# Softmax sums taken by ScalarE from the scores of the maxima, instead of by GpSimd and TensorE from the weights

## The chip, the core and the metric

One core of a Trainium2 chip runs the whole kernel. The metric is the device time of one execution in microseconds; the kernel before takes 1525.75 us (median of three runs, 1524.82 to 1526.85). The five engines each work through their own queue in order: TensorE (PE; its weight loads are listed as PEld), VectorE (DVE), ScalarE (ACT), GpSimd (POOL) and SyncE (SP), which here issues most transfers. TensorE writes its results into eight PSUM banks of 128 partitions by 512 float32 numbers.

## What is computed

```python
def reference(x, wq, wk, wv, wo, A, B, Wr, br):          # x: 4 x 1024 x 512, float32
    q, k, v = (x @ w.T as 16 heads of 32, for w in (wq, wk, wv))
    probs = softmax(einsum('bqhd,bkhd->bhqk', q, k))      # over the 1024 keys, no scaling
    x = layernorm(x + einsum('bhqk,bkhd->bqhd', probs, v) @ wo.T)
    logits = x @ Wr.T + br                                # 8 experts, the best one is taken
    h, y = einsum('nd,erd->ner', x, A), einsum('ner,eor->neo', h, B) / 64
    return layernorm(x + y[best expert] * softmax(logits)[best expert])
```

Four batches of 1024 tokens go through attention with 16 heads, a layer norm, a choice of one of eight experts of rank 64 for each token, and a second layer norm. All is float32. The softmax needs, for each query and head, the maximum of 1024 scores, the exps of the scores less that maximum (the weights), and the sum of these exps. The change is about where that sum is taken.

## The kernel before

The work is cut into units of one batch and four heads (32 columns each, so four heads fill 128 partitions): 16 units. Scores are made twice, in two layouts.

*For the maxima* (`scores`, L280): a step takes 128 queries and 512 keys, that is one half of the keys, of one unit. Four matmuls (L290), one for each head, write four banks with the queries on partitions, and VectorE reduces each bank to 128 negated maxima (L292). Every eight such steps fill a tile `top` of 2 x 128 queries x 4 heads x 2 halves; the smaller of the two negated maxima is taken (L296), GpSimd splits it into three bfloat16 parts (`split`, L190), which it writes into three of every 32 columns of the tile `spread_m`, and TensorE turns that tile (`turn_m`, L299), so that ScalarE can copy `mT` out: maxima on partitions, queries along the row.

*For the weights* (`weigh`, L313): 16 steps later, a step takes 256 queries and 256 keys of a unit, with the keys on partitions. In each of four banks, one matmul with ones (L321) spreads the negated maxima and two matmuls (L330) add the scores. ScalarE's exp (L340) turns the four banks into weights, `probs`. Here the keys lie on partitions, so a sum over keys goes across them: GpSimd adds the eight tiles of keys up into `dens` (L343, L351), all but the last one (or two).

*At the end of four steps* the 1024 keys of a chunk of 256 queries are done. `combine` (L364) multiplies the weights by the values into one bank (L372), and ScalarE copies it into half of a tile `both` (L380). Two steps later `settle` (L383) sums `dens` and the last weights across partitions by matmuls with ones (L360), and ScalarE copies that into the other half (L391); VectorE takes reciprocals (L394) at the end of that step and a step later GpSimd multiplies the halves (`divide`, L399) into `aT`, which the output projection needs.

The order on every engine is the order in which the program is written (`keep_order`). Step i of the loop at its end emits: transfers (`early`), small things that must come first (`ahead`), the weights of step i - 16, the scores of step i, the combine if step i - 16 ends a chunk (such steps are called `busy`), small work due at that step (`small`), the pieces that a planner has put there (`fill`) and small things that come last (`behind`). There are 256 + 16 steps. Weights and scores therefore run side by side in 240 of them; the first 16 have scores only and the last 16 weights only.

The planner (L913) deals out the pieces: projections to q, k and v of later units, each into one bank (`project_q`, `project_k`, `project_v`, copied out by ScalarE), the output projection with the first norm (`After.project`, `norm`), the experts (`After.step`; for the last batch `Last.up`, `mask`, `down`) and their norms. Costs are in TensorE columns: a step without a combine has 4 * 512 + 512 + 4 * 512 = 4608, a combine 8192, half a projection 4096. Pieces are added to a step that is not busy while its length and half the next piece stay below a level, which is at least `SHORTEST` = 8800 and more where deadlines (`last`) ask for it. Windows `first` and `last` say when a piece may and must run.

`bank()` gives out the eight banks in turn, whoever asks. A matmul into a bank waits until what was in it has been read.

`apply` (L419) is the second half of a layer norm, one ScalarE instruction with a scale and a bias for each partition, for 128 tokens of 512 numbers.

Of the kernel before, what the change touches and what calls it, by code (L numbers as in the profile page):

```python
# [41 lines left out]
def attention_then_experts(  # L42
# [89 lines left out]
    before_f = work.tile([P, P], F32, tag="both", name="before_f")  # L132
# [34 lines left out]

    spread_m = [const.tile([P, HT, GH, HD], BF16, tag=f"sm{i}", name=f"sm{i}") for i in range(2)]
# [3 lines left out]
    expand_f = work.tile([E, E, R], F32, tag="dens", name="expand_f")  # L172
# [36 lines left out]
    qT, kT, vS, mT, aT, top, probs, dens = {}, {}, {}, {}, {}, {}, {}, {}  # L209
# [43 lines left out]
    def project_q(u, x):  # L253

        ps = bank()[:, :QC]
        for c in range(C):
            pe.matmul(ps, wq_sb[:, c, ts(units[u][1], P)], x.x[:, c, :], start=(c == 0), stop=(c == C - 1))  # L257
        qT[u, x.n] = work.tile([P, QC], F32, tag="q", name="q", bufs=3 * NQ)
        act.copy(qT[u, x.n], ps)

    def project_k(u, x):

        if x.n == 0:
            kT[u] = work.tile([P, S], F32, tag="k", name="k", bufs=5)
        ps = bank()[:, :QC]
        for c in range(C):
            pe.matmul(ps, wk_sb[:, c, ts(units[u][1], P)], x.x[:, c, :], start=(c == 0), stop=(c == C - 1))  # L267
        act.copy(kT[u][:, ts(x.n, QC)], ps)

    def project_v(h, x, t):  # L270

        if x.n == 0 and t == 0:
            vS[x.b, h] = work.tile([P, NK, H2 + E], F32, tag="v", name="v", bufs=3)
        ps = bank()[:, : H2 + (E if h else 0)]
        for c in range(C):
            pe.matmul(ps, x.x[:, c, ts(t, P)], wv_sb[:, c, columns(h)], start=(c == 0), stop=(c == C - 1))  # L276
        act.copy(vS[x.b, h][:, x.n * TQ + t, : H2 + (E if h else 0)], ps)


    def scores(s):  # L280

        u, t, n = maxima[s]
        i, here = divmod(s, TS)
        if here == 0:
            top[i] = work.tile([P, HT, GH, 2], F32, tag="top", name="top")
        tiles = [bank() for _ in range(GH)]
        q = qT[u, t // TQ]
        for j, ps in enumerate(tiles):
            r = slice(j * HD, (j + 1) * HD)
            pe.matmul(ps, q[r, ts(t % TQ, P)], kT[u][r, ts(n, 512)], start=True, stop=True)  # L290
        for j, ps in enumerate(tiles):
            dve.tensor_reduce(top[i][:, here // 2, j, n : n + 1], ps, axis=AX.X, op=ALU.max, negate=True)  # L292
        if here == TS - 1:
            m = work.tile([P, HT, GH], F32, tag="m", name="m")
            parts = [spread_m[i % 2][:, :, :, p] for p in range(NP)]
            dve.tensor_reduce(m, top[i], axis=AX.X, op=ALU.min)  # L296
            split(m, parts, "mrest")
# [15 lines left out]
    def weigh(s):  # L313
# [27 lines left out]
        if kp == 0:  # L341
            dens[u, c] = work.tile([P, GH * QC], F32, tag="dens", name="dens")
            pool.tensor_add(  # L343
                dens[u, c],
                pr[:, 0].rearrange("p j q -> p (j q)"),
                pr[:, 1].rearrange("p j q -> p (j q)"),
            )
        else:
            for k in range(2):
                if 2 * kp + k < added(u):  # L350
                    pool.tensor_add(dens[u, c], dens[u, c], pr[:, k].rearrange("p j q -> p (j q)"))  # L351

    def added(u):

        return NK - 1 if u < U - 1 else NK - 2

    def sum_up(ps, tiles):
        for i, w in enumerate(tiles):
            for j in range(GH):
                pe.matmul(  # L360
                    ps[j * HD : (j + 1) * HD, :], ones, w[:, j, :], start=(i == 0), stop=(i == len(tiles) - 1)
                )

    def combine(u, c):  # L364

        b, g = units[u]
        ps = bank()
        v = vS[b, g // 2]
        for k in range(NK):
            for j in range(GH):  # L370
                col = (g % 2) * P + j * HD
                pe.matmul(  # L372
                    ps[j * HD : (j + 1) * HD, :QC],
# [5 lines left out]
        both = work.tile([P, 2 * QC], F32, tag="both", name="both")  # L379
        act.copy(both[:, :QC], ps[:, :QC])  # L380
        return both

    def settle(u, c, both):  # L383

        ps = bank()[:, :QC]
        sum_up(
            ps,
            [probs[u, c, k // 2][:, k % 2] for k in range(added(u), NK)]
            + [dens[u, c].rearrange("p (j q) -> p j q", q=QC)],
        )  # L390
        act.copy(both[:, QC:], ps)  # L391

    def invert(both):
        dve.reciprocal(both[:, QC:], both[:, QC:])  # L394

    def divide(u, c, both):
        b, g = units[u]
        aT[b, g, c] = work.tile([P, QC], F32, tag="aT", name="aT", bufs=16)
        pool.tensor_mul(aT[b, g, c], both[:, :QC], both[:, QC:])  # L399
# [19 lines left out]
    def apply(h, rs, i):  # L419
        act.activation(h, h, AF.Identity, bias=rs[:, 1, i : i + 1], scale=rs[:, 0, i : i + 1])  # L420
# [234 lines left out]
    class Last:  # L655
# [26 lines left out]
        def norm(self):  # L682
            for i in range(TQ):
                apply(self.h[i], self.rs, i)
# [63 lines left out]
    COST_S, COST_T, COST_AV = 4 * 512, 512 + 4 * 512, 4 * NK * QC  # L748
    HALF = 4 * C * QC
    SHORTEST = 8800  # L750
# [33 lines left out]
    summed = {}  # L784
    for i, (u, c, kp) in enumerate(weights):
        if kp == KP - 1:
            later(i + NS + 2, 2048, lambda u=u, c=c: settle(u, c, summed[u, c]))
            later(i + NS + 2, 0, lambda u=u, c=c: invert(summed[u, c]), where=behind)
            later(i + NS + 3, 0, lambda u=u, c=c: divide(u, c, summed[u, c]))
# [4 lines left out]
    for i in range(len(weights) // TS):  # L794
        later(TS * i + TS + 2, 512, turn_m, i)


    for u in range(1, LAST):
        for n in range(NQ):
            x_in = Load(units[u][0], n)  # L800
            first = max(start_of(u - 3) + KP * (n + 1), 0)
# [32 lines left out]
    for b, r in enumerate(rest):  # L834
# [7 lines left out]
        for t in range(NT):  # L842
            n, i = divmod(t, TQ)
            for half in range(2):
                then = []
                if i == TQ - 1 and half == 1:
                    then = [(2, 0, r.norm, n), (3, 0, r.choose, n), (4, 0, r.gate, n)]
                    if n == NQ - 1:
                        then += [(4, 600, r.count)]
                        then += [(5 + k // 4, 0, r.scatter, k) for k in range(NT)]  # L850
# [3 lines left out]
                    end - NS + KP * (n + 1) + 3,  # L854
                    end - NS + KP * (n + 1) + 8,
# [4 lines left out]
        for k in range(NT + 2):  # L860
# [3 lines left out]
                end + 14 + 3 * k,  # L864
                end + 21 + 3 * k,
                after=[(p, 3 if k else 9)],
                then=[(-1, 0, r.weigh_y, k - 2), (2, 0, r.norm_y, k - 2), (3, 0, r.store, k - 2)] if k >= 2 else [],
# [12 lines left out]
    for n in range(NQ):  # L880
        a = start_of(LAST) + NS * n + NS - 1
        p, ups, downs = None, [], []
        for i in range(TQ):
            for half in range(2):
                then = []
                if i == TQ - 1 and half == 1:
                    gap = 2 if n < NQ - 1 else 1
# [6 lines left out]
                    a + 4,  # L894
                    a + 9 if n < NQ - 1 else a + 5,
# [4 lines left out]
        for k in range(C):  # L900
            ups.append(Piece(on_last(n, "up", k), HALF, a + 8, a + 16, after=[(p, gap + 2)]))
        q = Piece(on_last(n, "mask"), 1024, a + 10, a + 18, after=[(p, gap + 3)] + [(o, 1) for o in ups])

        first = a + 12 if n != NQ - 2 else N + 5
        for i in range(TQ):
            for half in range(2):
                done = i == TQ - 1 and half == 1
                then = [(1, 0, on_last(n, "finish"))] if done else []
                Piece(on_last(n, "down", i, half), HALF, first, a + 22, after=[(q, 1)], then=then)
# [84 lines left out]
    for i in range(len(base)):  # L994
# [8 lines left out]
        if i in busy:  # L1003
            u, c, _ = weights[i - NS]
            summed[u, c] = combine(u, c)
# [43 lines left out]
```

## Time and profile before

| | |
|---|---|
| median of three runs | 1525.75 us |
| the profiled execution | 1532.2 us |
| its span, first to last instruction | 1530.5 us, granted TensorE clock 0.997 |
| first weights / last scores on TensorE | 99.8 us / 1407.8 us |
| PE busy | 1495.6 us (98%) |
| POOL busy | 1116.1 us (73%), of it the adds into dens 896.2 |
| DVE busy | 929.0 us (61%), of it the maxima 635.0 |
| ACT busy | 763.2 us (50%), of it the exps 528.8 |
| mean time of one multiply or add of 256 columns out of a bank by VectorE (L457) | 421 ns |
| mean time of one copy of 256 columns out of a bank by ScalarE (L380) | 373 ns |

A group of the profile gives line, engine, operation, tile written and tile read, shapes and count; then the busy time and the mean time of one in ns; then the idle time of the engine just before them and what ended it. A window line gives, for one stretch, the busy time and number of instructions of each engine (PE, PEld, DVE, ACT, POOL in this order), the granted clock and the DMA engines' share. A timeline line gives start, length, engine, line and operation, with equal neighbours merged. A busy TensorE counts pipelined matmuls whose ends are modelled, so instructions of one engine may overlap.

### The profile page before, as it was taken

What the parts mean: (1) busy time and instruction counts of PE and PEld (TensorE: products, weight loads), DVE (VectorE), ACT (ScalarE), POOL (GpSimd) and SP (SyncE); (2) the same over time, 40 slices, a digit from 0 to 9 for tenths busy, and PEclk for the clock granted to TensorE, in tenths of its full rate; (3) what the DMA queues carried; (4) which work ended last, traced back from release to release, by engine and by line L of the source; (5) the groups of instructions that cost most, each with busy time, mean ns of one, the idle gap of its engine ahead of it and who ended that gap; (6) DMA issues with size and microseconds to landing.
All of it is one profiled execution on the core that took longest, in us unless ns stands there. A gap on an engine that the chain in (4) does not pass through costs nothing.

```text
span 1530.5 us, 37870 instructions
## 1 busy us (share of the span) xinstructions
PE 1495.6 (98%) x15571; PEld 965.1 (63%) x15571; DVE 929.0 (61%) x1733; ACT 763.2 (50%) x1583; POOL 1116.1 (73%) x939
## 2 busy tenths in 40 slices
PE   8999999999999999999999999999999999999996
PEld 6666666666666666666666666666666565665655
DVE  1556666656676457666677556766667567776323
ACT  1125555554445556555445555655445455555551
POOL 2028888877777777888777868888877777778880
PEclk9999999999999999999999999999999999999999
DMA  7431212132002423324100522441400331121000
GB/s 234 138 102 51 71 43 71 42 97 99 15 15 97 146 84 111 113 90 146 35 15 30 173 84 77 125 139 43 166 15 16 123 93 33 57 82 61 29 1 28
DMA packets 93054, 122.13 MB, mean 80 GB/s; under 512 B 7608, under 2 KB 68040, under 8 KB 92881
## 3 DMA queue, kind: packets, MB, share of 16 engines
q1 hardware_dynamic: 84672, 103.93, 21.6%
q0 software_dynamic: 6096, 13.69, 2.4%
q8 instruction: 122, 2.00, 0.6%
q10 hardware_dynamic: 2112, 2.10, 0.4%
q14 instruction: 52, 0.42, 0.1%
HBM read 92.34 MB, written 33.63 MB: 82 GB/s over the span
## 4 chain that ended last, share of the span: by engine, by line
PE 88%; POOL 4%; ACT 3%; issue 2%; DVE 2%; DMA 1%; ACTq 0%; POOLq 0%; SPq 0%; DVEq 0%
PE bank L372 14%; PE bank L290 14%; PE bank L330 13%; PE bank L276 8%; PE bank L257 8%; PE bank L267 8%; PE bank L455 7%; PE bank L321 5%; PE bank L360 4%; POOL dens L351 3%; ACT probs L340 2%; PE bank L601 2%; PE bank L617 2%; PE bank L608 2%; PE bank L729 1%
## 5 line engine op out<-in xcount | busy, mean ns | idle before, releaser
L292 DVE TENSOR_REDUCE top<-bank 128x1 f32<-128x512 f32 x1024 | 635.0, 682 | 458.9 <-PE bank L290 451.9
L351 POOL TENSOR_TENSOR dens<-dens,probs 128x1024 f32<-128x1024 f32 x316 | 745.3, 2358 | 128.7 <-ACT probs L340 116.4
L340 ACT ACTIVATE probs<-bank 128x512 f32<-128x512 f32 x1024 | 528.8, 603 | 286.2 <-PE bank L330 272.9
L290 PE MATMUL bank<-k,q 32*128 32x512 f32 x2048 | 287.1, 594 | 1.5 <-DVE whose_i L552 1.3
L330 PE MATMUL bank<-q,k 32*128 32x256 f32 x4096 | 266.9, 374 | 0.0
L372 PE MATMUL bank<-probs,v 128*32 128x256 f32 x4096 | 236.0, 381 | 0.8 <-ACT probs L340 0.8
L330 PEld LDWEIGHTS bank<-q,k 32*128 32x128 f32 x4096 | 201.4, 184 | 18.8 <-issue 3.2
L372 PEld LDWEIGHTS bank<-probs,v 128*32 128x32 f32 x4096 | 127.1, 110 | 125.9 <-ACT probs L340 47.9
L343 POOL TENSOR_TENSOR dens<-probs 128x1024 f32<-128x1024 f32 x64 | 150.9, 2358 | 62.7 <-ACT probs L340 62.4
L257 PE MATMUL bank<-xT,wq 128*128 128x256 f32 x512 | 129.2, 398 | 8.7 <-DMA xT<-in_xt 6.1
L290 PEld LDWEIGHTS bank<-k,q 32*128 32x128 f32 x2048 | 112.0, 184 | 25.8 <-issue 6.1
L267 PE MATMUL bank<-xT,wk 128*128 128x256 f32 x512 | 125.4, 389 | 1.4 <-ACT probs L340 0.9
L276 PE MATMUL bank<-wv,xT 128*128 128x256 f32 (+1 forms) x512 | 125.0, 391 | 0.6 <-ACT probs L340 0.2
L257 PEld LDWEIGHTS bank<-xT,wq 128*128 128x128 f32 x512 | 95.2, 194 | 47.4 <-ACT probs L340 25.7
L455 PE MATMUL bank<-wo,aT 128*128 128x264 f32 (+1 forms) x512 | 123.2, 389 | 1.7 <-POOL aT L399 1.7
L394 DVE RECIPROCAL both<-both 128x256 f32<-128x256 f32 x64 | 111.6, 1744 | 11.1 <-ACT both L391 11.1
L276 PEld LDWEIGHTS bank<-wv,xT 128*128 128x128 f32 x512 | 93.7, 190 | 36.6 <-ACT probs L340 18.9
L267 PEld LDWEIGHTS bank<-xT,wk 128*128 128x128 f32 x512 | 95.3, 192 | 33.8 <-ACT probs L340 21.1
L455 PEld LDWEIGHTS bank<-wo,aT 128*128 128x128 f32 x512 | 94.5, 190 | 32.8 <-ACT probs L340 16.8
L321 PE MATMUL bank<-mT,ones_b 3*128 3x512 bf16 x1024 | 107.5, 384 | 3.1 <-ACT probs L340 1.5
L380 ACT COPY both<-bank 128x256 f32<-128x256 f32 x64 | 23.9, 373 | 157.6 <-PE bank L372 151.6
L635 POOL DMA_INDIRECT out<-x x48 | 49.5, 1032 | 53.8 <-DMA out<-x 35.3
(124 smaller groups left out, 1038.4 us busy)
## 6 DMA issues: line engine op xcount, KB each, us to landing
xT<-in_xt SPq DMA_DIRECT2D x98, 512.0 KB, 3.6
sorted<-nothing SPq DMA_DIRECT2D x12, 1028.0 KB, 7.4
x<-sorted SPq DMA_DIRECT2D x48, 257.0 KB, 3.0
h<-in_x SPq DMA_DIRECT2D x32, 256.0 KB, 4.6
wa<-in_wa SPq DMA_DIRECT2D x48, 128.0 KB, 2.6
wb<-in_wb SPq DMA_DIRECT2D x48, 128.0 KB, 3.6
out<-h SPq DMA_DIRECT2D x8, 256.0 KB, 2.0
wo<-in_wo POOLq DMA_DIRECT2D x1, 1024.0 KB
```

The lines of the kernel that those rows point to most:

```text
L257: pe.matmul(ps, wq_sb[:, c, ts(units[u][1], P)], x.x[:, c, :], start=(c == 0), stop=(c == C - 1))
L267: pe.matmul(ps, wk_sb[:, c, ts(units[u][1], P)], x.x[:, c, :], start=(c == 0), stop=(c == C - 1))
L276: pe.matmul(ps, x.x[:, c, ts(t, P)], wv_sb[:, c, columns(h)], start=(c == 0), stop=(c == C - 1))
L290: pe.matmul(ps, q[r, ts(t % TQ, P)], kT[u][r, ts(n, 512)], start=True, stop=True)
L292: dve.tensor_reduce(top[i][:, here // 2, j, n : n + 1], ps, axis=AX.X, op=ALU.max, negate=True)
L321: pe.matmul(ps.rearrange("p (k q) -> p k q", q=QC), ones_b[r, :], m[r, :].unsqueeze(1).to_broadcast((NP, 2, QC)), start=True, stop=False,)
L330: pe.matmul(ps[:, ts(k, QC)], kT[u][r, ts(2 * kp + k, P)], qT[u, c][r, :], start=False, stop=(k == 1),)
L340: act.activation(pr[:, :, j, :], ps.rearrange("p (k q) -> p k q", q=QC), AF.Exp)
L343: pool.tensor_add(dens[u, c], pr[:, 0].rearrange("p j q -> p (j q)"), pr[:, 1].rearrange("p j q -> p (j q)"),)
L351: pool.tensor_add(dens[u, c], dens[u, c], pr[:, k].rearrange("p j q -> p (j q)"))
L372: pe.matmul(ps[j * HD : (j + 1) * HD, :QC], v[:, k, col : col + HD], probs[u, c, k // 2][:, k % 2, j, :], start=(k == 0), stop=(k == NK - 1),)
L455: pe.matmul(ps, aT[b, c, n][:, ts(i, P)], wo_sb[:, c, columns(half)], start=(c == 0), stop=(c == C - 1))
```

## The change

The sums are no longer made from the weights. In `scores`, after VectorE's maximum of a bank, ScalarE runs an exp over the same bank, with that half's negated maximum as its bias, and writes the sum of the row out (`accum_out`) into a tile `sums`; the exps themselves go into one bfloat16 tile, `junk`, which nobody reads. So there are two sums per query and head, one for each half of the keys. After eight steps, VectorE and ScalarE make the corrections exp(maximum of the half - maximum of all); in the new `invert`, at the beginning of the next step, VectorE multiplies, adds the halves and takes the reciprocal, and GpSimd splits maxima and reciprocals together, into six columns of `spread_m` instead of three. `turn_m` is as before and turns both. In `combine`, four matmuls with a constant `pick`, which has ones where the reciprocals' parts lie, spread the reciprocals over the 32 partitions of each head; VectorE copies them into `inv` and multiplies the combined values by them straight from the bank. `settle`, `divide`, the old `invert`, the tiles `dens` and `both`, and GpSimd's adds are gone.

Beside that, VectorE instead of ScalarE copies q, k and v out of their banks; the norms go from ScalarE to GpSimd, but for the last chunk of the last batch; q has 16 buffers instead of 12; and the planner has a floor of 10600, wider windows for q and k, and shorter gaps behind a combine. A few constants take other buffers while they are made.

```diff
+    pick_f = work.tile([P, GH, HD], F32, tag="hT", name="pick_f")
+    pool.memset(pick_f, 1.0)
+    for base_, sign in ((1 - NP, 1), (2 * NP, -1)):
+        pool.affine_select(out=pick_f, in_=pick_f, compare_op=ALU.is_gt, fill=0.0, base=base_,
+                           pattern=[[-sign * HD, GH], [0, HD]], channel_multiplier=sign)
+    pick = const.tile([P, GH, HD], BF16, tag="pick", name="pick")
+    pool.tensor_copy(pick, pick_f)
+    junk = const.tile([P, 512], BF16, tag="junk", name="junk")
...
     def project_q(u, x):
...
-        qT[u, x.n] = work.tile([P, QC], F32, tag="q", name="q", bufs=3 * NQ)
-        act.copy(qT[u, x.n], ps)
+        qT[u, x.n] = work.tile([P, QC], F32, tag="q", name="q", bufs=4 * NQ)
+        dve.tensor_copy(qT[u, x.n], ps)
...
     def scores(s):
...
+            sums[i] = work.tile([P, HT, GH, 2], F32, tag="sums", name="sums")
...
+        most, total = (a[i][:, here // 2, :, n : n + 1] for a in (top, sums))
         for j, ps in enumerate(tiles):
-            dve.tensor_reduce(top[i][:, here // 2, j, n : n + 1], ps, axis=AX.X, op=ALU.max, negate=True)
+            dve.tensor_reduce(most[:, j], ps, axis=AX.X, op=ALU.max, negate=True)
+        for j, ps in enumerate(tiles):
+            act.activation(junk, ps, AF.Exp, bias=most[:, j], accum_out=total[:, j])
         if here == TS - 1:
-            m = work.tile([P, HT, GH], F32, tag="m", name="m")
-            parts = [spread_m[i % 2][:, :, :, p] for p in range(NP)]
-            dve.tensor_reduce(m, top[i], axis=AX.X, op=ALU.min)
-            split(m, parts, "mrest")
+            m = work.tile([P, HT, GH, 2], F32, tag="m", name="m")
+            less = work.tile([P, HT, GH, 2], F32, tag="less", name="less")
+            dve.tensor_reduce(m[:, :, :, 0], top[i], axis=AX.X, op=ALU.min)
+            dve.tensor_sub(less, m[:, :, :, 0:1].to_broadcast((P, HT, GH, 2)), top[i])
+            act.activation(less, less, AF.Exp)
+            room[i] = m, less
+
+    def invert(i):
+        m, less = room[i]
+        dve.tensor_mul(less, less, sums[i])
+        dve.tensor_reduce(m[:, :, :, 1], less, axis=AX.X, op=ALU.add)
+        dve.reciprocal(m[:, :, :, 1], m[:, :, :, 1])
+        split(m, [spread_m[i % 2][:, :, :, p : 2 * NP : NP] for p in range(NP)], "mrest")
...
     def weigh(s):
...
-        if kp == 0:
-            dens[u, c] = work.tile([P, GH * QC], F32, tag="dens", name="dens")
-            pool.tensor_add(dens[u, c], ...)
-        else:
-            for k in range(2):
-                if 2 * kp + k < added(u):
-                    pool.tensor_add(dens[u, c], dens[u, c], pr[:, k].rearrange("p j q -> p (j q)"))
...
-    def combine(u, c):
+    def combine(s):
+        u, c, _ = weights[s]
...
+        ps = bank()[:, :QC]
+        for j in range(GH):
+            pe.matmul(ps[j * HD : (j + 1) * HD, :], pick[:, j, :], mT[s // TS][:, ts(s % TS // KP, QC)],
+                      start=True, stop=True)
+        inv = work.tile([P, QC], F32, tag="inv", name="inv")
+        dve.tensor_copy(inv, ps)
...
-        both = work.tile([P, 2 * QC], F32, tag="both", name="both")
-        act.copy(both[:, :QC], ps[:, :QC])
-        return both
...
         aT[b, g, c] = work.tile([P, QC], F32, tag="aT", name="aT", bufs=16)
-        pool.tensor_mul(aT[b, g, c], both[:, :QC], both[:, QC:])
+        dve.tensor_mul(aT[b, g, c], ps, inv)
...
-    def apply(h, rs, i):
-        act.activation(h, h, AF.Identity, bias=rs[:, 1, i : i + 1], scale=rs[:, 0, i : i + 1])
+    def apply(h, rs, i, eng=pool):
+        scale, shift = rs[:, 0, i : i + 1], rs[:, 1, i : i + 1]
+        if eng is act:
+            act.activation(h, h, AF.Identity, bias=shift, scale=scale)
+        else:
+            eng.tensor_scalar(h, h, scale, shift, ALU.mult, ALU.add)
...
-    COST_S, COST_T, COST_AV = 4 * 512, 512 + 4 * 512, 4 * NK * QC
+    COST_S, COST_T, COST_AV = 4 * 512, 512 + 4 * 512, 4 * NK * QC + QC
-    SHORTEST = 8800
+    SHORTEST = 10600
...
-            later(i + NS + 2, 2048, lambda u=u, c=c: settle(u, c, summed[u, c]))
-            later(i + NS + 2, 0, lambda u=u, c=c: invert(summed[u, c]), where=behind)
-            later(i + NS + 3, 0, lambda u=u, c=c: divide(u, c, summed[u, c]))
...
+        later(TS * i + TS, 0, invert, i, where=ahead)
         later(TS * i + TS + 2, 512, turn_m, i)
...
-            first = max(start_of(u - 3) + KP * (n + 1), 0)
+            first = max(start_of(u - 4) + KP * (n + 1), 0)
...
-                    then = [(2, 0, r.norm, n), (3, 0, r.choose, n), (4, 0, r.gate, n)]
+                    then = [(1, 0, r.norm, n), (2, 0, r.choose, n), (3, 0, r.gate, n)]
...
-                    end - NS + KP * (n + 1) + 3,
-                    end - NS + KP * (n + 1) + 8,
+                    end - NS + KP * (n + 1),
+                    end - NS + KP * (n + 1) + 6,
...
-                end + 14 + 3 * k,
-                end + 21 + 3 * k,
-                after=[(p, 3 if k else 9)],
+                end + 11 + 3 * k,
+                end + (18 + 4 * k if b < B - 2 else 18 + 3 * k),
+                after=[(p, 3 if k else 8)],
```

Windows of the last batch's pieces move in the same way, by two to five steps.

## The prediction

> **What bounds the kernel now.** I read the page first, then the stretches between the first softmax weight and the last score, then the groups and one step of the timeline. The first line is the page's busy time. The next three are busy times by stretch: the lead (scores and projections only, 0 to 99.8 us), the joint stretch in which every step has both weights and scores (240 steps), and the tail (16 steps without scores, then the last tokens).
>
> ```profile
> PE 1495.6 (98%) x15571; PEld 965.1 (63%) x15571; DVE 929.0 (61%) x1733; ACT 763.2 (50%) x1583; POOL 1116.1 (73%) x939
> ```
>
> ```profile
> 0.00:99.80 99.80, 93.70 (x500) 68.21 (x504) 37.55 (x62) 16.45 (x42) 10.63 (x77) 1.00 0.51 164
> 99.80:1407.80 1308.00, 1297.60 (x14067) 825.50 (x14060) 850.65 (x1575) 692.07 (x1432) 1028.63 (x797) 1.00 0.25 79
> 1407.80:1530.50 122.70, 104.30 (x1013) 71.40 (x1007) 40.82 (x97) 54.69 (x109) 76.81 (x66) 0.97 0.06 19
> ```
>
> TensorE (first busy number of a stretch) fills 1297.6 of 1308 us, so a joint step of 5.45 us is its own instructions end to end; ScalarE (fourth) fills 692. What TensorE loses is time saved, as long as nothing else then needs more than about 5.2 us a step. The same windows for the settle matmuls (L360) alone, first the joint stretch, then the tail:
>
> ```profile
> 99.80:1407.80 1308.00, 64.03 (x960) 25.14 (x960) 1.00 0.25 79
> 1407.80:1530.50 122.70, 7.04 (x96) 2.20 (x96) 0.97 0.06 19
> ```
>
> The groups that price the new work (mean ns after the comma), then a ScalarE and a GpSimd piece of the timeline (start, length):
>
> ```profile
> L340 ACT ACTIVATE probs<-bank 128x512 f32<-128x512 f32 x1024 | 528.8, 603 | 286.2 <-PE bank L330 272.9 <-ACT xsT L602 4.2 <-PE bank L290 2.6
> L321 PE MATMUL bank<-mT,ones_b 3*128 3x512 bf16 x1024 | 107.5, 384 | 3.1 <-ACT probs L340 1.5 <-DVE top L292 0.7
> L420 ACT ACTIVATE h<-h,rs 128x512 f32<-128x512 f32 x40 | 30.6, 825 | 29.1 <-POOL rs L410 29.1
> L602 ACT COPY xsT<-bank 128x512 f32<-128x512 f32 x48 | 25.8, 593 | 23.8 <-PE bank L601 23.8
> L436 ACT ACTIVATE ex<-bank 128x16 f32<-128x16 f32 x16 | 3.0, 188 | 15.8 <-DVE bank L434 15.8
> ```
>
> ```profile
> 612.18 2.07 ACT L340 ACTIVATE probs<-bank 128x512 f32<-128x512 f32 x4 [0.86 <-PE bank L330]
> ```
>
> ```profile
> 4.75 0.52 POOL L164 MEMSET nothing<- 128x514 f32 x1
> 5.33 0.10 POOL L165 MEMSET nothing<- 128x1 int32 x1
> 5.36 0.53 POOL L170 MEMSET sm<- 128x512 bf16 x1
> ```
>
> Four exps take 2.07 us though each lasts 0.603: they start (2.07-0.603)/3 = 0.49 us apart, overlapping by 0.11. L165 overwrites part of what L164 has just written: it starts 0.06 us after L164's end. L170 writes another tile and starts 0.03 us after L165 began. So a second write to the same tile by the same engine waits for the first to finish.
>
> **What goes.** TensorE loses L360, 64 us in the joint stretch and 7 in the tail. GpSimd loses the dens adds (745.3 + 150.9 us) and divide (46.9); it gains up to 84 norms of 0.5 us (a 128x514 memset, L164) to 1.2 us (half the 2.36 us of the 128x1024 add), at most 100 us, so it ends near 270 us and no wait on it counts. ScalarE loses in the joint stretch both (22.0 + 23.5), q, k and v (19.8 + 19.9 + 18.1) and norms (56.7): 692 - 160 = 532 us stay, 538 with thirty small exps of L436's 0.19.
>
> **What comes on TensorE.** 60 groups of four bf16 pick matmuls of 256 columns. Four of 512 columns (L321) take 4 x 0.105 = 0.42 us; half of that, 0.2, is the lower end, and 0.45 the upper (half the 1.0 us of L360's eight fp32 ones). I take 0.3: 18 us. TensorE needs 1308 - 64 + 18 = 1262 us there.
>
> **What comes on VectorE.** About 154 q/k/v copies and 60 of inv at 0.37 (ScalarE's row, the nearest), 60 multiplies at 0.42 (L457), small work of some 1 us per group of maxima (30), less the reciprocals (102.9): 850 + 79 + 25 + 30 - 103 = 881 of 1308 us. Not a bound. The multiply waits in VectorE's queue for the combine, and behind it stand only reduces of scores which TensorE issues after that combine. The new `invert` stands ahead of a step's reduces and waits for ScalarE's small exp of the corrections. That costs nothing while ScalarE is the later one anyhow; without that cover it is one exp, 0.19 us, thirty times, 6 us.
>
> **What comes on ScalarE decides.** 960 exps over scores in the joint stretch, of an unseen kind: a bias from SBUF, a sum written out, and all into one tile, `junk`. Step by step: 0.603 for the row of the same shape. A pointer operand: the norm L420 has two and lasts 825 against 593 for the copy L602 with none, so 0.116 each. A write into junk right behind the last one: no overlap, plus 0.06 as for L165. The sum: between nothing and a whole small instruction, 0.188 (L436); I take 0.074, L436 less the 0.114 of overlap, because a short instruction behind a long one should overlap it as exps do. That is 0.603 + 0.116 + 0.06 + 0.074 = 0.85 us. The first of each four stands behind a weights' exp, so saves 0.17. Mean (0.68 + 3 x 0.85)/4 = 0.81. The ends: 0.49 (a plain exp, as L340) and 0.92 (full 0.188). ScalarE then needs 538 + 960 x 0.81 = 1316 us, more than TensorE's 1262.
>
> The Trainium skill, "ScalarE: Activation LUTs", section "What ACT_TABLE_LOAD costs", gives about 93 ns for a pointer operand where the rows here give 116. The same skill's "VectorE: DVE Perf Modes", section "The DRAIN you can't avoid", found that a semaphore after each op costs nothing extra; that speaks against my 0.17 for the wait on junk, and the L164/L165 rows (another engine) speak for it. By both rules an exp would be 0.66 us, ScalarE's joint stretch 1172, and TensorE would stay the bound.
>
> **Banks.** The eight PSUM banks go round in order. A step takes four for weights, four for scores and k for the rest. The next weights then need k banks of the scores, which are now free only after VectorE's maximum and ScalarE's exp. With k up to 2 ScalarE still has two exps to do, 1.6 us, while TensorE makes the next weights (1.1 us: L321 at 610.83, first score matmul at 611.92), so it does not run dry. From k = 3 it does. Counting matmul groups between weights, with two per combine as after the change and no settle, 40 of the 240 steps have k of 3 or more. At 0.3 to 1 us each that is 12 to 40; I take 25.
>
> **The planner.** Windows and waiting steps shift, as no settle stands between combine and projection; loads and stores move by a step or so on queues that are mostly idle (SP's DMA share 0.25). The floor of 10600 still admits one piece: 4608 + 4096 = 8704, and half a piece more is 10752. Early steps, now 4.0 to 5.7 us apart in TensorE's starts, thus may stay short of what ScalarE needs, 5.5; this only matters where TensorE would otherwise be the bound.
>
> **Tail and sum.** The tail loses the 7.0 of L360. At its end GpSimd's adds, the reciprocal and the divide hold the projection until 1489.15, while the combine ends at 1483.7; up to 5 us go, plus or minus picks. Between 5 and 12, I take 7.7: 115. Sum in the profiled run: 99.8 + 1316 + 25 + 115 + 1.7 outside the span (1532.2 - 1530.5) = 1557.5, against 1532.2. The median of the runs is 0.9958 of that: 1551 us.
>
> **Rivals.**
> 1. TensorE stays the bound. If junk brings no wait, an exp is 0.49 + 0.116 + 0.074 = 0.68, ScalarE needs 538 + 653 = 1191 and hides. Then 99.8 + 1262 + 115 + 1.7 = 1478.5; with the early short steps (ScalarE's 5.0 against TensorE's 4.5 in about 48, 22 us) 1500. Median 1472 to 1494, 1486 taken. For it: ScalarE's large idle time now; against it: L164/L165. It turns at 0.78 us an exp: (1308 + 7.7 of the tail - 25 - 538)/960. Chance 0.36.
> 2. ScalarE at full price: a mean of 0.92 makes 538 + 883 = 1421, and banks at 40: 1677, median 1670. From 1610 up I count it here. For it: the sum must come out of a long pipeline after the last element. Chance 0.14.
> 3. A balance: exps at 0.77 to 0.79 leave the time where it is. Chance 0.06, 0.04 of it within 0.2% (3 us, about what measurement tells from no change), 0.02 below.
>
> The forecast, 1529 to 1610, has 0.44. Slower 0.44 + 0.14 = 0.58, same 0.04, faster 0.38. Both signs hold much; the forecast's own range is 1530 to 1605. The whole range, 1472 to 1640, leaves out most of rival 2 and a little below rival 1.
>
> **What would show it.** Right: new exps start 0.8 to 0.9 us apart within a four, ScalarE over 95% busy in the joint stretch, TensorE near 94% there (1262 of 1341) with its idle time released by ScalarE's exps over scores, VectorE near 67%, GpSimd under 20%. Wrong: new exps 0.7 us apart or closer, with TensorE still at 98%; or ScalarE below 90% while TensorE waits too, which would be the banks.

## The result, and the profile after

The change makes the kernel slower: 1632.66 us (median of four runs, 1619.48 to 1635.08) against 1525.28 for the kernel before on the same chip (four runs, 1524.59 to 1526.85). The ratio is 1.0685, interval 1.0626 to 1.0743. The forecast was 1551: the sign is right, and the loss is 107 us where 26 were forecast. The profiled execution took 1634.17 us, its span 1632.4, its mean granted TensorE clock 0.984 (before: 0.997).

The page's busy line, and then the stretches, cut as they were for before: the lead, the joint stretch of 240 steps with weights and scores, the tail. Columns: length, then busy time of TensorE, its weight loads, VectorE, ScalarE and GpSimd, the granted clock, the DMA share and GB/s.

```profile
PE 1580.1 (97%) x14771; PEld 1002.7 (61%) x14771; DVE 979.3 (60%) x2117; ACT 1353.4 (83%) x3259; POOL 248.3 (15%) x583
```

```profile
0.00:104.30 104.30, 96.39 (x516) 70.24 (x516) 56.40 (x111) 51.21 (x132) 11.75 (x81) 1.00 0.50 162
104.30:1525.20 1420.90, 1389.64 (x13341) 865.15 (x13341) 890.90 (x1912) 1254.14 (x3027) 222.09 (x470) 0.98 0.23 73
1525.20:1632.40 107.20, 94.09 (x920) 67.32 (x915) 32.04 (x95) 48.08 (x102) 14.48 (x33) 0.97 0.06 21
```

The forecast for this execution was 1557.5. Lead 104.3 and tail 107.2 are 4.5 over and 7.8 under. The joint stretch took 1420.9 where 1341 stood, and there lie the missing 80 us. In it no engine looks like the bound that was forecast: ScalarE is busy for 1254 us, 88%, and TensorE appears to be at 98% though it has fewer matmuls than before (14771 against 15571 in the span).

The groups show what hides there (total busy us, mean ns; then the idle time ahead of the group and what ended it). The first row is the score matmuls in the kernel before, the others are of the kernel after:

```profile
L290 PE MATMUL bank<-k,q 32*128 32x512 f32 x2048 | 287.1, 594 | 1.5 <-DVE whose_i L552 1.3
L314 ACT ACTIVATE junk<-bank,top 128x512 bf16<-128x512 f32 x1024 | 710.5, 694 | 77.9 <-DVE top L312 53.0
L309 PE MATMUL bank<-k,q 32*128 32x512 f32 x2048 | 394.7, 616 | 2.7 <-DVE whose_i L560 2.7
L314 ACT ACTIVATION_READ_ACCUMULATOR junk<-bank,top 128x1 f32 x1024 | 207.5, 203 | 0.0
L354 PE MATMUL bank<-mT,ones_b 3*128 3x512 bf16 x1024 | 145.8, 382 | 25.2 <-ACT junk L314 18.5 <-ACT probs L373 0.2
```

The score matmuls (L309) are the same 2048 as before, where they were L290 with 287.1 us busy; the ones-matmuls (L354) were L321 with 107.5. The 146 us more are not more matmuls. The record of a single matmul is hardly longer (616 ns against 594), but these are the first matmuls to write into banks that ScalarE's exps still hold, and they start further apart. Their records overlap less, and a pause shorter than a record does not show as idle time. Two rows of the waits, for the pauses that do show, look at it from both ends (us in total, times, longest):

```profile
PEld bank L309 <- ACT junk L314: 50.1, 110, 0.5
ACT probs L373 <- PE bank L363: 150.3, 165, 4.9
```

TensorE waits for ScalarE's exps over scores, and elsewhere ScalarE waits 150 us, 134 of them in the joint stretch, for the matmuls that make the weights' scores. Each waits for the other, in different steps. A ScalarE that bounded the stretch would not wait.

### The profile page after: what moved, and what is told of

The parts are those of the page before. It is cut to its first block, busy times and chain, and to the rows that moved or that the text cites. A ratio compares the mean times of both kernels' runs of the same rounds, so it can differ in the third digit from the quotient of the medians.

```text
span 1632.4 us, 38436 instructions
## 1 busy us (share of the span) xinstructions
PE 1580.1 (97%) x14771; PEld 1002.7 (61%) x14771; DVE 979.3 (60%) x2117; ACT 1353.4 (83%) x3259; POOL 248.3 (15%) x583
## 4 chain that ended last, share of the span: by engine, by line
PE 83%; DVE 8%; ACT 5%; issue 2%; DMA 1%; SPq 0%; POOL 0%; ACTq 0%; POOLq 0%; DVEq 0%
PE bank L309 19%; PE bank L395 14%; PE bank L363 13%; PE bank L274 7%; DVE top L312 7%; PE bank L463 6%; PE bank L284 6%; PE bank L293 6%; PE bank L354 5%; ACT probs L373 3%; ACT junk L314 2%; PE bank L722 2%; PE bank L737 2%; DMA xT<-in_xt 1%; PE bank L381 1%
## 5 line engine op out<-in xcount | busy, mean ns | idle before, releaser
L312 DVE TENSOR_REDUCE top<-bank 128x1 f32<-128x512 f32 x1024 | 643.3, 683 | 306.6 <-PE bank L309 300.1
L314 ACT ACTIVATE junk<-bank,top 128x512 bf16<-128x512 f32 x1024 | 710.5, 694 | 77.9 <-DVE top L312 53.0
L309 PE MATMUL bank<-k,q 32*128 32x512 f32 x2048 | 394.7, 616 | 2.7 <-DVE whose_i L560 2.7
L363 PE MATMUL bank<-q,k 32*128 32x256 f32 x4096 | 280.6, 380 | 0.0
L314 ACT ACTIVATION_READ_ACCUMULATOR junk<-bank,top 128x1 f32 x1024 | 207.5, 203 | 0.0
L309 PEld LDWEIGHTS bank<-k,q 32*128 32x128 f32 x2048 | 158.9, 186 | 78.6 <-ACT junk L314 50.1
L354 PE MATMUL bank<-mT,ones_b 3*128 3x512 bf16 x1024 | 145.8, 382 | 25.2 <-ACT junk L314 18.5
L354 PEld LDWEIGHTS <-ones_b 3*128 3x128 bf16 x1024 | 32.7, 91 | 119.9 <-issue 118.8
L209 POOL CAST sm<-m 128x32 bf16<-128x32 f32 x32 | 8.2, 256 | 610.6 <-PE bank L363 408.9
L403 DVE TENSOR_TENSOR aT<-bank,inv 128x256 f32<-128x256 f32 x64 | 27.1, 424 | 110.9 <-PE bank L395 106.7
```

The source lines that it names most:

```text
L312: dve.tensor_reduce(most[:, j], ps, axis=AX.X, op=ALU.max, negate=True)
L314: act.activation(junk, ps, AF.Exp, bias=most[:, j], accum_out=total[:, j])
L354: pe.matmul(ps.rearrange("p (k q) -> p k q", q=QC), ones_b[r, :], m[r, :].unsqueeze(1).to_broadcast((NP, 2, QC)), start=True, stop=False,)
L363: pe.matmul(ps[:, ts(k, QC)], kT[u][r, ts(2 * kp + k, P)], qT[u, c][r, :], start=False, stop=(k == 1),)
```

## The theories

The theories have letters in the expectations. In short: **A**, the banks of the scores are held by the exps, and TensorE is late by that. **B**, ScalarE's total is what counts: take enough of it away, wherever, and TensorE's 1480 to 1510 appear. **C**, TensorE's own new order (picks, windows) costs more than was reckoned. **D**: every step costs the longer of what TensorE and what ScalarE have to do in that step. The eight banks hold just one step of weights and scores, so neither engine can use a short step to get ahead for a long one.

## Experiments

### Without the new exps: what TensorE alone needs

```
-        for j, ps in enumerate(tiles):
-            act.activation(junk, ps, AF.Exp, bias=most[:, j], accum_out=total[:, j])
+            pool.memset(sums[i], 1.0)      # where sums[i] is created
```

> The change without its 1024 exps over the scores; the sums are set to 1, so the softmax is not normalised. Theory A (the exps over scores hold banks, and TensorE and ScalarE then wait for each other in turn) and theory B (ScalarE simply has too much work): TensorE is the bound again, 1472 to 1500 us by the sum of the prediction. Theory C (the loss comes from what else the change moves: copies to VectorE, norms to GpSimd, the plan): above 1525 us.

Measured: 1489.34 us, ratio 0.9758 (0.9741 to 0.9774), clock 0.995. Everything but the exps thus gains 37 us, 3 us from rival 1's 1486, and C falls. In this kernel the 240 joint steps take 1282 us (1262 was forecast for TensorE, between marks some 5 us closer together), but far from evenly, by the starts of their ones-matmuls: 83 take under 5.0 us, 75 between 5.0 and 5.9, 82 more than that. A pair of them on TensorE's timeline (start, length, instructions):

```profile
264.26 0.40 PE L353 MATMUL bank<-mT,ones_b 3*128 3x512 bf16 x4
...
268.67 0.40 PE L353 MATMUL bank<-mT,ones_b 3*128 3x512 bf16 x4
268.89 1.03 PE L362 MATMUL bank<-q,k 32*128 32x256 f32 x16
269.76 1.02 PE L310 MATMUL bank<-k,q 32*128 32x512 f32 x8
...
274.75 0.40 PE L353 MATMUL bank<-mT,ones_b 3*128 3x512 bf16 x4
```

A short step of 4.41 us and one with a combine of 6.08. The same two steps in the kernel after, on TensorE and then on ScalarE:

```profile
289.79 0.39 PE L354 MATMUL bank<-mT,ones_b 3*128 3x512 bf16 x4
...
294.14 0.90 PE L354 MATMUL bank<-mT,ones_b 3*128 3x512 bf16 x4
294.67 1.23 PE L363 MATMUL bank<-q,k 32*128 32x256 f32 x16
295.64 2.25 PE L309 MATMUL bank<-k,q 32*128 32x512 f32 x8
...
301.50 0.39 PE L354 MATMUL bank<-mT,ones_b 3*128 3x512 bf16 x4
```

```profile
291.07 2.06 ACT L373 ACTIVATE probs<-bank 128x512 f32<-128x512 f32 x4 [1.00 <-PE bank L363]
...
295.46 0.69 ACT L314 ACTIVATE junk<-bank,top 128x512 bf16<-128x512 f32 x1
...
296.14 0.58 ACT L344 CAST mT<-bank 128x512 bf16<-128x512 f32 x1
296.60 2.07 ACT L373 ACTIVATE probs<-bank 128x512 f32<-128x512 f32 x4
...
302.79 1.09 ACT L373 ACTIVATE probs<-bank 128x512 f32<-128x512 f32 x2 [1.01 <-PE bank L363]
```

ScalarE needs 5.53 us for the first step (291.07 to 296.60) and TensorE 4.41: TensorE stands at the head of the next step, with groups of matmuls of 0.90, 1.23 and 2.25 us instead of 0.40, 1.03 and 1.02. In the second step ScalarE has 6.19 less 1.01 idle = 5.18 us of work and TensorE 6.08: now ScalarE waits. The pair takes 11.72 us. The totals are 10.49 for TensorE and 10.71 for ScalarE; the longer one of each step, added up, is 5.53 + 6.08 = 11.61. That is D in one pair.

Over all 240 steps, take TensorE's time from this kernel and ScalarE's work from the kernel after, counted as in the pair: from the first exp of a step's weights to that of the next step, less idle time of more than 0.15 us. The longer of the two in each step adds up to 1412 us, below called D's sum; the joint stretch took 1427 by the same marks. The totals are 1282 for TensorE and 1283 for ScalarE (1260 if the gaps of under 0.15 us between its instructions are left out too).

### One output tile for each of the four exps

```
+    junk = [const.tile([P, 512], BF16, tag=f"junk{j}", name=f"junk{j}") for j in range(GH)]
-            act.activation(junk, ps, ...)
+            act.activation(junk[j], ps, ...)
```

> Four tiles junk instead of one, so that no exp over scores has to wait for the one before it. The same starts should go from 0.81 us apart to 0.67 to 0.70 (0.69 for the exp less 0.1 of overlap, and the read of the sum with 0.09). That takes 720 x 0.12 = 86 us off ScalarE's 1254 in the joint stretch. Theory B: the time falls by all of it, to about 1545. Theory A: by less, as only steps in which ScalarE is the later one get shorter, 1560 to 1590. Theory C: no change.

Measured: 1587.79 us, ratio 1.0408 (1.039 to 1.0425), some 45 us less than after and no more. First the kernel after, then this kernel, on ScalarE's timeline inside a four:

```profile
603.98 0.69 ACT L314 ACTIVATE junk<-bank,top 128x512 bf16<-128x512 f32 x1
604.56 0.20 ACT L314 ACTIVATION_READ_ACCUMULATOR junk<-bank,top 128x1 f32 x1
604.79 0.69 ACT L314 ACTIVATE junk<-bank,top 128x512 bf16<-128x512 f32 x1
```

```profile
599.76 0.72 ACT L314 ACTIVATE junk<-bank,top 128x512 bf16<-128x512 f32 x1
600.33 0.24 ACT L314 ACTIVATION_READ_ACCUMULATOR junk<-bank,top 128x1 f32 x1
600.42 0.73 ACT L314 ACTIVATE junk<-bank,top 128x512 bf16<-128x512 f32 x1
```

The pitch falls from 0.81 to 0.66 us (medians over 768 pairs 812 and 663 ns). So writing the same tile again costs 0.15 us an exp: with one tile the next exp starts 0.03 us after the end of the read, with four it starts 0.09 us after the read began. This is the very price at which rival 1 put the end of the story (0.68 an exp, 1472 to 1494 us), and it is 100 us off: the failing step is not the price of an exp. D's sum for this kernel is 1365 us, 47 less than for the kernel after; its joint stretch took 1378, 49 less.

### The exps read a constant tile instead of the banks

```
+    flat = const.tile([P, 512], F32, tag="flat", name="flat")      # zeros
-            act.activation(junk, ps, AF.Exp, bias=most[:, j], accum_out=total[:, j])
+            act.activation(junk, flat, AF.Exp, bias=most[:, j], accum_out=waste[:, j : j + 1])
```

> The exps over scores read a constant tile in SBUF instead of the bank (so the sums are not the scores' and are replaced by 1): the same ScalarE work, the same wait for the maximum, but a bank of scores is free as soon as VectorE has its maximum. Theory A: ScalarE and TensorE no longer hold each other up, and the time falls to what the busier one needs: 104 + 1254 to 1290 + 107, so 1465 to 1510. Theory B: ScalarE has the same work, no change, 1620 to 1635.

Measured: 1639.43 us, ratio 1.0745 (1.0727 to 1.0763). The scores' banks come free with VectorE's maximum here, and nothing is gained. A, as stated, falls. TensorE now stands two instructions on, at a copy that ScalarE has queued behind its exps (the bracket holds the idle time and its releaser):

```profile
1010.16 0.39 PE L358 MATMUL bank<-mT,ones_b 3*128 3x512 bf16 x2
1011.74 0.54 PE L358 MATMUL bank<-mT,ones_b 3*128 3x512 bf16 x2 [1.19 <-ACT mT L348]
```

The exps start 0.85 us apart, so ScalarE has somewhat more to do; D's sum is 1425, measured 1431.

### Two rings of four banks

```
+    turn_of = {"w": 0, "s": 0}
+    def bank(ring="w"):
+        turn_of[ring] += 1
+        return banks[(turn_of[ring] - 1) % 4 + (4 if ring == "s" else 0)]
-        tiles = [bank() for _ in range(GH)]          # scores
+        tiles = [bank("s") for _ in range(GH)]
```

> Four of the banks are kept for scores; weights and all pieces take turns in the other four. The next weights then never wait for an exp over scores. If in theory A it is the order in which banks go round that hurts, the time falls by half of the loss or more, to 1575 or less. If it is that any bank of scores is held long, scores then wait for scores of the step before, and the time stays within 20 us of 1633. Theory B: no change.

Measured: 1885.97 us, ratio 1.2367 (1.2347 to 1.2388), clock 0.943. No theory had this. Weights, transposes, combines and projections now share four banks; a transpose waits for a copy that ScalarE has behind the exps of the weights.

```profile
714.28 0.66 PE L609 MATMUL bank<-ident,x 128*128 128x128 f32 x4 [1.76 <-ACT u L620]
```

It tells only that the rest needs the scores' banks too.

### Leave the exps out of 80 steps: the shortest, or the longest

Steps are ordered by TensorE's time in the kernel without the new exps. Both versions take the same 320 exps from ScalarE.

```
-        for j, ps in enumerate(tiles):
+        if s not in LEFT_OUT:
+            for j, ps in enumerate(tiles):
```

> As the change, but the four exps over scores are left out in 80 of the 240 joint steps (their sums are set to 1): in the 80 in which TensorE alone has least to do, 4.0 us a step on average between starts of weights in the run without any such exps. Theory D (new: TensorE cannot run ahead of ScalarE from one step to the next, so a step costs the longer of TensorE's own time and ScalarE's own time, 5.3 us, in that step, and a long step gives nothing back): summed over the steps, 121 us less, about 1510. Theory B (the sum of ScalarE's work): 80 x 3.2 = 256 us less of it than 1254, so TensorE is the bound, 1480 to 1510.

> The same number of exps over scores left out, but in the 80 joint steps in which TensorE alone has most to do (6.1 us and more, 6.5 on average). ScalarE's work falls by the same 256 us. Theory B: the same time as with the short steps left out, 1480 to 1510. Theory D: no gain, as in these steps ScalarE was not the later one: 1620 to 1635.

Measured: out of the short steps 1524.28 us, ratio 0.9948 (0.9931 to 0.9964); out of the long ones 1638.06, ratio 1.0696 (1.0672 to 1.072). The pages' busy lines, the short ones first:

```profile
PE 1475.8 (97%) x14771; PEld 960.8 (63%) x14771; DVE 970.7 (64%) x2117; ACT 1123.1 (74%) x2619; POOL 249.5 (16%) x615
```

```profile
PE 1576.9 (97%) x14771; PEld 1000.8 (61%) x14771; DVE 979.3 (60%) x2117; ACT 1116.1 (68%) x2619; POOL 248.5 (15%) x615
```

ScalarE's work is the same within 7 us, and about 235 us less than after. One version is some 110 us faster than after, the other gains nothing. This decides between B and D: ScalarE's total doesn't matter, only its work in steps in which TensorE has less to do. With the exps out of the short steps the pair shown above takes 4.35 and 6.02 us, as if there were no exps at all. D's sums for the two are 1304 and 1411, measured 1319 and 1428.

### The opposite: a fifth exp in 80 steps

```
+        if s in TWICE:
+            act.activation(junk, tiles[3], AF.Exp, bias=most[:, 3], accum_out=total[:, 3])
```

> As the change, but in the 80 joint steps in which TensorE alone has most to do (6.1 us and more) the last of the four exps over scores is run twice: 80 x 0.81 = 65 us more for ScalarE. Theory D (a step costs the longer of the two): 2 to 4 us more, so 1633 to 1640. If the loss were a matter of ScalarE's total, 65 us more, 1698.

> The same 65 us more of ScalarE, but in the 80 steps in which TensorE alone has least to do. Theory D: ScalarE is the later one in each of them, so all of it shows: 1698. If only the total counted: the same as with the long steps.

Measured: in the long steps 1641.31 us, ratio 1.0762 (1.0744 to 1.078); in the short ones 1726.91, ratio 1.1325 (1.1306 to 1.1344).

```profile
PE 1586.4 (97%) x14771; PEld 1008.0 (62%) x14771; DVE 979.3 (60%) x2117; ACT 1412.1 (86%) x3419; POOL 247.4 (15%) x583
```

```profile
PE 1637.8 (95%) x14771; PEld 1013.7 (59%) x14771; DVE 981.2 (57%) x2117; ACT 1415.7 (82%) x3419; POOL 248.2 (14%) x583
```

About 60 us more work for ScalarE costs some 10 us in long steps and 94 in short ones. D's sums rise by 2 and by 65; the sign and the place are D's, but the 94 are some 30 more than the work itself. The granted clock is 0.958 to 0.965 there, against 0.985 to 0.990 with the fifth exp in long steps.

### ScalarE's copies on VectorE

mT, xsT and u, which ScalarE copies out of PSUM, go to VectorE; alone, with four junk tiles, and with the constant tile as source.

```
-                act.copy(mT[i], ps)                 # likewise xT[k] and u[k]
+                dve.tensor_copy(mT[i], ps)
```

> Three copies go from ScalarE to VectorE: the turned maxima (mT), the turned tokens of the experts (xsT) and u, 58 us of ScalarE. In ScalarE's queue they stand behind the exps over scores, and their banks are needed by the next weights. Theory D: the steps that have them need up to 7 us of ScalarE; the sum of the longer ones falls by 46 us, to about 1587. If only the total of ScalarE counts, 58 us, 1575. If the copies were hidden, no change.

> Four junk tiles and the three copies on VectorE together. Theory D: ScalarE's part of a step falls to some 4.7 us, the sum of the longer ones by 76 us, and by the 13 that four junk tiles gave beyond their sum: 1545 to 1560. Still above 1525, as the steps of 4.0 us stay too short.

> Which link carries ScalarE's lateness to TensorE. Either of two may hold TensorE in the step after a short one: the last banks of scores, free only after their exp (away in the run with the constant tile, no gain), and the banks of mT, xsT and u, copied out by ScalarE behind these exps (away in the run with the three copies on VectorE, no gain). Here both are away (exps over a constant tile, sums set to 1, copies on VectorE). If the two links stand in for each other, TensorE can now run ahead and a long step pays for a short one: towards the larger of the totals, 1282 in the joint stretch, 1500 to 1560 in all. If a third link (the weights' own banks) holds it as well, 1610 to 1640 again.

Measured: alone 1634.35, ratio 1.0655 (1.062 to 1.0689); with four tiles 1587.03, ratio 1.0362 (1.0341 to 1.0383), by the ratio 7 us less than four tiles without the copies' move. Both fell short of what was expected by 30 to 50 us. VectorE has the time on average, but not in those steps, which also hold its own statistics. Its timeline, and what ScalarE meets next:

```profile
1012.66 1.27 DVE L610 COPY xsT<-bank 128x512 f32<-128x512 f32 x2
...
1015.87 2.47 DVE L312 TENSOR_REDUCE top<-bank 128x1 f32<-128x512 f32 x4
```

```profile
1016.64 0.69 ACT L314 ACTIVATE junk<-bank,top 128x512 bf16<-128x512 f32 x1 [0.91 <-DVE top L312]
```

VectorE works from 1008.15 to 1018.67 almost without a break, so the maxima come late and ScalarE's exps wait for them: here the wait moved to a third engine. That explains a part at most. Over the whole run these waits grew from 53 us in 24 cases to 63 us in 42, while D's sum with the copies off ScalarE is 1374 us and the joint stretch took 1427 (with four tiles 1337 and 1378). The rest of the miss is open.

With the constant tile as well 1606.63, ratio 1.0529 (1.0511 to 1.0546): some 25 us less than after, though each of the two edits alone gained next to nothing. TensorE did not run ahead for it: D's sum is 1386 us here, 26 less than for the kernel after, and the joint stretch took 1400. With both links away a step still costs the longer of the two, so something else ties the engines as well. In the stretch shown it is a bank of the weights themselves:

```profile
1016.29 0.40 PE L385 MATMUL bank<-mT,pick 128*32 128x256 bf16 x4 [1.01 <-ACT probs L377]
```

### Even steps

The combine of a chunk, four steps' weights at once in the kernel after, is cut in parts: at each step the eight matmuls for the step before, into a bank kept for that. The ring of the rest has seven. The planner's costs and a window of the projections to v move with it.

```
-        for k in range(NK):
+        for k in (2 * kp, 2 * kp + 1):
-        base[i + NS] += COST_AV                       # once a piece
+        base[i + NS + 1] += COST_AV // KP             # at each step
```

> To even out TensorE's steps: the combine's 32 matmuls, so far all in every fourth step, are dealt out, eight a step, between the weights and the scores, each time for the weights of the step before; they add up in one bank that is kept for them, and the planner's costs follow. Here without the exps over scores (sums set to 1), to see TensorE alone: the same work, so 1480 to 1500 as before the dealing, if seven banks for the rest are enough.

> The same dealt-out combine with the exps over scores and one junk tile, nothing else changed against the change. Theory D: a step has 4.65 us of TensorE with one piece and 6.35 with two (2.05 + 0.9 + 1.7 a piece), against ScalarE's 5.3. With 38% of two pieces the mean of the longer is 5.7 a step, 1368 in the joint stretch against 1421 of the change: 1570 to 1590. Theory B: no change, 1625 to 1640.

> Dealt-out combine and four junk tiles. Theory D: ScalarE's 4.9 us a step against 4.65 and 6.35: 5.45 a step, 1308 in the joint stretch, 1510 to 1535, about the time of the kernel before. Theory B: 1588, as with four junk tiles alone.

> The same and the three copies on VectorE, which gave nothing by themselves. Theory D: 4.7 us a step, 5.33 on average, 1278 in the joint stretch: 1490 to 1530, if VectorE does not get in the way; if it does, as with the copies alone, no gain over the last one.

Measured: without the exps 1542.07, ratio 1.0107 (1.009 to 1.0123); with them 1723.57, ratio 1.1285 (1.1264 to 1.1305); with four tiles 1672.84, ratio 1.0955 (1.0936 to 1.0973); with the copies on VectorE too 1676.5, ratio 1.0983 (1.0964 to 1.1001). All four missed, and D's simple sum with them: the steps became even (half of them between 5.19 and 5.50 us without the exps), D's sum with the exps fell to 1368, and the joint stretch took 1517. Ring of seven and dealt-out combine together cost 53 us before any of the new exps is run (1542 against 1489); no run tells the two apart. With the exps two waits grow:

```profile
ACT junk L316 <- DVE top L314: 231.1, 253, 21.7
...
PE bank L356 <- ACT junk L316: 66.3, 210, 1.4
```

With seven banks the next weights need one more bank that an exp over scores may still hold; TensorE waits for it 210 times (47 times in the kernel after). ScalarE waits for maxima 253 times (24). What evenness is worth by itself stays unmeasured, since no bank is left over to give to it.

## Why the forecast was wrong, and its sign right by luck

- **The price of a new exp: right.** Forecast 0.85 us apart within a four, measured 0.81. Its parts: the exp itself lasts 694 - 605 = 89 ns longer than one over weights, which is put down to the pointer operand (116 was taken). The Trainium skill, "ScalarE: Activation LUTs", section "What ACT_TABLE_LOAD costs", has about 93 ns for one pointer operand, and this trace sides with it. The sum is an instruction of its own of 203 ns, of which 0.09 us is left after overlap (0.074 was taken). The second write into junk costs 0.15 (0.17 was taken). The same skill's "VectorE: DVE Perf Modes", section "The DRAIN you can't avoid", finds on VectorE that a semaphore after each op costs nothing extra. On ScalarE, here, writing the same tile again does cost something: 0.81 against 0.66 us. ScalarE's joint total came out at 1254, 62 below the 1316: the 960 exps and their sums take 750 us and not 778, the rest some 504 and not 538.
- **TensorE's part: right.** Picks 19.0 us (18), joint stretch alone 1282 (1262). VectorE 63% (67%), GpSimd 248 us (near 270). The tail took 107.2 (115).
- **The step that failed is the sum of the joint stretch.** It set ScalarE's total against TensorE's, took the larger, ScalarE's, as the bound, and put all that the two could cost each other at 25 us, from 40 steps with three or more other groups. It had seen that TensorE's steps differ (4.0 to 5.7 us) and that the planner admits that, and set it aside with "this only matters where TensorE would otherwise be the bound". It matters most where two engines' totals are close: with 1282 us for TensorE and 1283 for ScalarE by the same marks, the longer of each step adds up to 1412, so unevenness costs some 130 us, five times the 25. ScalarE was no bound: it was busy for 88% of the stretch, where over 95% was forecast.
- **The sign was luck.** The forecast put ScalarE's total 62 us too high, and that hid a part of the other error. With 1282 as the larger total, the same sum gives 104.3 + 1282 + 25 + 107.2 + 1.7 = 1520 for the profiled execution, against 1532 before: faster.
- **What D's sum leaves over** is 6 to 17 us for the kernel after, four tiles, the constant tile (alone and with the copies moved), both versions without 80 steps' exps and the fifth exp in long steps. A part may be the lower granted clock: the run of the kernel after with the clock at 0.994 took 1619.48 us, the other three, at 0.984 or 0.985, 1631.15 to 1635.08. That is an association; nothing here set the clock by itself. Where D's sum leaves over more, it is not the whole account: 38 us with the fifth exp in short steps, 53 and 41 with the copies on VectorE, some 150 with the dealt-out combine and the exps, 220 with two rings.
- **Rival 1** turned on whether junk brings a wait. It fell by its own condition being met, in the run with four tiles. **Rival 2** has the measured time in its range, from 1610 up, but not for its reason: it took an exp at a mean of 0.92 us and ScalarE's total at 1421, and the runs show 0.78 (750 us for 960) and 1254. Its argument, that the sum must come out after the last element, weighs little here: the read of the sum begins before its exp ends, and 0.09 us of it is left. **The signs named in advance** worked: "ScalarE below 90% while TensorE waits too" is what the profile shows, 88%. It was put down there to the banks. The waits name the banks too, but freeing the scores' banks alone gave nothing, and no run takes the whole tie away: that each step costs the longer of the two is shown, that the banks are the tie is argued from the waits and from the order of the program.
- **Open:** how much each of the three links (the scores' banks, those of the three copies, the weights' own) is worth once the others are gone, and whether two steps of run-ahead would bring the full difference to 1489. That wasn't tried: it needs eight more banks.

None of the versions that keep the sums beats the kernel before; the best of these are the two with four output tiles, 1587 and 1588 us.

## What to carry to other kernels

Where two engines work in lockstep through a small ring of buffers, add up the longer of the two step by step, not the two totals; near balance the difference is the whole result. Work that is to hide on another engine must fit into each step's own slack: here the same 320 exps were worth some 110 us in short steps and nothing in long ones. And read a bound by what waits, not by its busy share: here TensorE's busy time grew by 146 us without more matmuls, mostly pauses: one shorter than a matmul's record leaves no gap. Compare the busy time of the same matmuls, or the time from step to step, with a version that does not wait.

## What the runs showed of the hardware that was not expected

- The granted TensorE clock is lower in the versions with more waits, but not in proportion: 0.997 before, 0.995 without the exps, 0.984 after, 0.965 with the fifth exp in short steps, 0.943 with two rings; but also 0.984 with the dealt-out combine and the exps, which takes 90 us more than after. It falls to half for a few us at a time. In the joint stretch of the kernel after it does so eight times, for 3.4 or 6.8 us, 44 us in all. Two stretches of 50 us, and the one of half rate within the second (columns as above, the clock third from the end):

```profile
650.00:700.00 50.00, 48.55 (x486) 28.32 (x485) 31.49 (x63) 45.53 (x111) 8.30 (x16) 1.00 0.36 106
950.00:1000.00 50.00, 48.48 (x460) 29.59 (x460) 28.43 (x56) 43.75 (x107) 6.57 (x15) 0.93 0.19 59
963.90:970.70 6.80, 6.80 (x48) 3.24 (x44) 3.00 (x5) 6.67 (x16) 0.00 (x0) 0.50 0.06 21
```

- A ScalarE exp from SBUF in fp32 is a little longer than one from PSUM: 726 ns against 694, and 0.85 us apart against 0.81.
- The read of the sum begins before its exp ends (0.58 us into an exp of 0.69). With four output tiles the next exp in turn starts 0.09 us after the read began, so it was the shared tile, more than the sum, that kept the exps apart.
